# The router of a mixture of experts in five pieces, its places with five products, and a PSUM bank for each tile of an expert's output

## The chip, the cores and the metric

The kernel runs on one core of a Trainium2 chip, as one program. The metric is the device time of an execution in microseconds; lower is better. The core has TensorE for matrix products (PE in the profile), VectorE (DVE), ScalarE (ACT), GpSimd (POOL) and a queue for transfers, SyncE (SP). Each engine works through its own list of instructions; they wait for each other by semaphores. Products are written to PSUM[...] and DVE or ACT copies them out.

## The reference

The input is 8 batches of 512 tokens with 256 features. Two decoder layers follow each other, each with self-attention, attention with a context, and a feed-forward part, with a normalisation after each. The last two parts are where the change is:

```python
x = _layernorm(x + _L1_xattn_ref(x, ctx_1024, L1_xattn_Wq1, ..., L1_xattn_bo), axis=-1)
x = _layernorm(x + _L1_ffn_ref(x, L1_ffn_gamma, L1_ffn_beta, L1_ffn_router_w, L1_ffn_W1, L1_ffn_W2), axis=-1)
```

The attention with the context has 8 heads of 64 features; each token attends to the 512 tokens of its batch and 64 context tokens. The feed-forward part is a mixture of 8 experts:

```python
xn = (x - mu) * jax.lax.rsqrt(var + EPS) * gamma + beta
logits = jnp.einsum('btd,ed->bte', xn, router_w)
probs = jax.nn.softmax(logits / TEMP, axis=-1)
w, idx = jax.lax.top_k(probs, K)
wdense = jnp.sum(jax.nn.one_hot(idx, E, dtype=w.dtype) * w[..., None], axis=-2)
h = jax.nn.silu(jnp.einsum('btd,edf->betf', xn, W1))
y = jnp.einsum('betf,efd->betd', h, W2)
out = jnp.einsum('bte,betd->btd', wdense, y)
return out + res
```

With K = 2, E = 8, and 1,024 hidden features of each expert. Each token's result needs its two chosen experts only.

## The kernel before

Everything is in 32-bit floats. The core goes through the parts one after the other; in each, batches, heads and blocks of 128 tokens are the units of a software pipeline. The helper `_pipeline` (L32) runs a list of units through a list of stages with delays: in each step, one unit stands in every stage. At the end of a step it takes one function from a list of work put off (`put_off`, or `last_route` in the last part) and calls it, which puts that function's instructions at this place in the program.

**The context attention of the second layer** ("l1_context") has 8 x 4 x 4 = 128 units (batch b, pair of heads c, block of 128 tokens i). In each step TensorE makes the scores of one unit (`l1x_scores`: s_sc, L1077 and L1079), transposes the probabilities of the unit two steps earlier (`l1x_transposes`: tP2 L1092, tP L1097, each evacuated by `evac`, which takes DVE at L108 and ACT at L110 in turn), multiplies with the values of the unit six steps earlier (`l1x_values`: o_pv L1109), and does a piece of the next head pair's projections (`l1x_project`: t_qk L1034, copied by ACT into q or by DVE into k, L1039; t_v L1044), or, once per batch, the transposes of the next batch's x (`l1x_share`: xT, through tT L198). DVE takes the maxima (nm, L1081) and scales by the sums (L891, L893); ACT takes the exponentials (L1082). In this stage TensorE's instructions keep the order of the program (`tc.manual_schedule(engines={PE})`); the other engines' are ordered by the compiler's scheduler.

When the fourth head pair of a batch is done, `out_done` (L943) puts off two pieces of the output projection (`project_and_norm`: o_out L239, added to x and bias at L246, and after the second piece the normalisation `normed`, L213 to L223, whose power runs on POOL at L216), and `routed` puts off the batch's router, four pieces with an empty one ahead of each:

- `route_norm`: the experts' normalisation, into the tile `z`, which also holds the two weights of each token and its number; x doubled (L1165), and written to the array `total` in memory. The pool that holds `z` has one buffer for it.
- `route_transposes`: z is transposed (tZ, L1175) and scaled with gamma and beta on ACT (L1176) into xnT, one of the two buffers with the tag xT, which x's own transposes use too.
- `route_picks`: eight products give the logits (o_r, L1190); softmax and the two largest of eight follow on DVE with one exponential on ACT (L1198 to L1221). At L1221 the token numbers are copied into z.
- `route_places`: each chosen token's place in its expert's region is the number of tokens before it with the same choice, counted by products of the 0/1 matrix of choices `both` with a strictly triangular matrix `under` (the same block of 128 tokens) and one of ones (the blocks before): 14 products for o_rank (L1229, L1231, L1233), the last four for the new counts. Then the row numbers (irow), and eight indirect transfers, each of 128 rows, from z to the experts' input `rows_in` (L1245), issued by POOL.

Batch 6 is followed by `early_blocks`, which makes on DVE the table of which expert each of the first units has, and the load of the first unit. Batch 7 keeps its router for the next part, where `last_route` holds it, with two empty pieces after the first.

**The experts** ("l1_experts") work in 39 units, 32 pairs of 128-row tiles, in which each unit's tiles share an expert, and seven single tiles. A unit is loaded (`moe_load`: its cells of the table, xr L1368 and weights L1369 and L1370, by SP), two steps later transposed (`moe_pre`, tZ), then multiplied with the first weights (`moe_up`: s_h L1402) and the second (`moe_down`: o_y L1419). Its rows are scaled with their weights (L1439) and added to `total` by indirect transfers (L1440). The tail loads `total` (L1487), normalises it and writes it out.

PSUM in these parts: two tiles of two banks for s (s_sc, s_h), three of one bank for t (tP2, tP, tT, tZ, t_qk, t_v, and, through `u_tile`, o_out, o_r, o_rank, o_y), and one for o_pv. A tile waits until the reader of the tile that had its bank is done.

Of the kernel before, what the change touches and what calls it, by code (L numbers as in the profile page):

```python
# [11 lines left out]
F32 = mybir.dt.float32  # L12
I32 = mybir.dt.int32
AF = mybir.ActivationFunctionType
ALU = mybir.AluOpType
AX = mybir.AxisListType
PSUM = bass.MemoryType.PSUM

P = 128
S = 512  # L20
D = 256
S2 = 64
NT = S // P
# [5 lines left out]
TILES = 2  # L29
# [20 lines left out]
def decoder_kernel(ctx: ExitStack, tc: tile.TileContext, a: dict, out: bass.AP):  # L50
    nc = tc.nc
    NB = a["x"].shape[0]
    NE = a["mo_w1"].shape[0]
# [9 lines left out]
    pe, act, dve, pool, sp = nc.tensor, nc.scalar, nc.vector, nc.gpsimd, nc.sync  # L63
# [3 lines left out]
    work = ctx.enter_context(tc.tile_pool(name="work", bufs=2))  # L67
# [24 lines left out]
    def t_tile(name):  # L92
        return pp["t"].tile([P, 4, P], F32, tag="t", name=name)

    def o_tile(name):
        return pp["o"].tile([P, 512], F32, tag="o", name=name)

    def u_tile(name):

        return t_tile(name).rearrange("p i n -> p (i n)") if pp["one"] else o_tile(name)  # L100
# [89 lines left out]
    hmask, rev = small[:, 0:8], small[:, 8:16]  # L190
# [165 lines left out]
    live = {}  # L356
# [192 lines left out]
    with tc.tile_pool(name="bfly", bufs=1, side="right") as bfly, phase("l0_self") as ph, psum("a", 3, 1, 1):  # L549
# [10 lines left out]
        o = o_tile("o_wlat")  # L560
        for c in range(KC):
            for k in range(KC):
                pe.matmul(
                    o[:, c * 64 : (c + 1) * 64],
                    lhsT=wkT[:, k, c * P : (c + 1) * P],
                    rhs=wdown[:, k, :],
                    start=(k == 0),
                    stop=(k == KC - 1),
# [53 lines left out]
        o = o_tile("o_bias")  # L622
# [167 lines left out]
    with phase("l0_context_ffn") as ph:  # L790
# [10 lines left out]
        for f in range(0, 8, 2):  # L801
# [8 lines left out]
            pieces=2,  # L810
# [84 lines left out]
    put_off = []  # L895
# [103 lines left out]
    for c in range(4):  # L999
        o = u_tile("o_k2")  # L1000
        for kc in range(KC):
            pe.matmul(
                o[:, 0:NC2],
                lhsT=wk2[:, kc, c * P : (c + 1) * P],
                rhs=ctxT[:, kc, :],
                start=(kc == 0),
                stop=(kc == KC - 1),
# [124 lines left out]
    ones = keep.tile([P, P], F32, name="ones")  # L1132
    under = keep.tile([P, P], F32, name="under")
# [15 lines left out]
    def e_tile(name):  # L1149
        return work.tile([P, NT, NE], F32, tag=name, name=name, bufs=1)  # L1150

    def e_col(name):
        return work.tile([P, NT], F32, tag=name, name=name, bufs=1)

    def over_e(c):
        return c.unsqueeze(2).to_broadcast([P, NT, NE])

    def over_i(c):
        return c.unsqueeze(1).to_broadcast([P, NT, NE])
# [22 lines left out]
            )  # L1182
        live["xnT", b] = xnT

    def route_picks(b):
        xnT = live.pop(("xnT", b))
        o = u_tile("o_r")[:, 0 : NT * NE].rearrange("p (i e) -> p i e", e=NE)
        for i in range(NT):
            for c in range(KC):
                pe.matmul(  # L1190
                    o[:, i, :],
                    lhsT=xnT[:, c, i * P : (i + 1) * P],
                    rhs=rw[:, c, :],
                    start=(c == 0),
                    stop=(c == KC - 1),
                )
        pr, top, hit, rest = e_tile("pr"), e_col("top"), e_tile("hit"), e_tile("rest")
        dve.tensor_reduce(top, o, AX.X, ALU.max)  # L1198
        dve.tensor_tensor(pr, o, over_e(top), ALU.subtract)
        act.activation(pr, pr, AF.Exp, scale=1.0 / 1.5)  # L1200
        dve.tensor_reduce(top, pr, AX.X, ALU.add)
        dve.reciprocal(top, top)
        dve.tensor_tensor(pr, pr, over_e(top), ALU.mult)

        left = pr
        picks = []
        for k in range(2):
            pick = e_tile(f"pick{k}")
            dve.tensor_reduce(top, left, AX.X, ALU.max)
            dve.tensor_tensor(hit, left, over_e(top), ALU.is_equal)  # L1210
            dve.tensor_tensor(hit, hit, over_i(rev), ALU.mult)
            dve.tensor_reduce(top, hit, AX.X, ALU.max)
            dve.tensor_tensor(pick, over_i(rev), over_e(top), ALU.is_equal)
            if k == 0:
                dve.scalar_tensor_tensor(rest, pick, -2.0, pr, ALU.mult, ALU.add)
                left = rest
            picks.append(pick)
        both, z = e_tile("both"), live["z", b]
        dve.tensor_tensor(both, picks[0], picks[1], ALU.add)
        dve.tensor_tensor(z[:, :, D : D + NE], both, pr, ALU.mult)  # L1220
        dve.tensor_copy(z[:, :, D + NE], tokens_at[:, b * NT : (b + 1) * NT])  # L1221
        live["picks", b] = picks, both

    def route_places(b):

        picks, both = live.pop(("picks", b))
        o = u_tile("o_rank")
        for i in range(NT):
            pe.matmul(o[:, i * NE : (i + 1) * NE], lhsT=under, rhs=both[:, i, :], start=True, stop=(i == 0))  # L1229
            for j in range(i):  # L1230
                pe.matmul(o[:, i * NE : (i + 1) * NE], lhsT=ones, rhs=both[:, j, :], start=False, stop=(j == i - 1))  # L1231
        for i in range(NT):
            pe.matmul(o[:, NT * NE : (NT + 1) * NE], lhsT=ones, rhs=both[:, i, :], start=(i == 0), stop=(i == NT - 1))  # L1233
        rank, hit, place = e_tile("rank"), e_tile("hit"), e_col("place")
        dve.tensor_tensor(rank, o[:, 0 : NT * NE].rearrange("p (i e) -> p i e", e=NE), over_i(count), ALU.add)
        dve.tensor_tensor(rank, rank, over_i(region), ALU.add)
        dve.tensor_tensor(count, o[:, NT * NE : (NT + 1) * NE], count, ALU.add)
        z = live.pop(("z", b))
        for k in range(2):
            dve.tensor_tensor(hit, picks[k], rank, ALU.mult)  # L1240
            dve.tensor_reduce(place, hit, AX.X, ALU.add)
            row = work.tile([P, NT], I32, tag=f"irow{k}", name="irow", bufs=2)
            dve.tensor_copy(row, place)
            for i in range(NT):
                pool.indirect_dma_start(  # L1245
                    out=rows_in[:, :],
                    out_offset=bass.IndirectOffsetOnAxis(ap=row[:, i : i + 1], axis=0),
                    in_=z[:, i, :],
                    in_offset=None,
                )  # L1250
# [161 lines left out]
    def moe_down(n):  # L1412
        _, mine, size = where[n]
        h = live.pop(("h", n))
        xr, _, w2, cells = live.pop(("load", n))
        o = u_tile("o_y").rearrange("p (i n) -> p i n", i=TILES)
        for i in range(size):
            for f in range(8):
                pe.matmul(  # L1419
                    o[:, i, :],  # L1420
                    lhsT=h[:, f, i * P : (i + 1) * P],
                    rhs=w2[:, f, :],
                    start=(f == 0),
                    stop=(f == 7),
                )

        wt = ph.tile([P, TILES, NE], F32, tag="wt", name="wt", bufs=2)[:, 0:size]
        share = ph.tile([P, TILES], F32, tag="share", name="share", bufs=2)[:, 0:size]
        to = ph.tile([P, TILES], I32, tag="to", name="to", bufs=4)[:, 0:size]
        tc.keep_in_program_order(  # L1430
            dve.tensor_tensor(wt, xr[:, :, D : D + NE], mine.unsqueeze(1).to_broadcast([P, size, NE]), ALU.mult)
        )
        dve.tensor_reduce(share, wt, AX.X, ALU.add)
        tc.keep_in_program_order(dve.tensor_copy(to, xr[:, :, D + NE]))
        y = ph.tile([P, TILES, D], F32, tag="y", name="y", bufs=3)

        tc.keep_in_program_order(dve.tensor_copy(y[0:1, 0, 0:2], cells))
        for i in range(size):
            dve.tensor_scalar(y[:, i, :], o[:, i, :], share[:, i : i + 1], None, ALU.mult)  # L1439
            pool.indirect_dma_start(  # L1440
                out=total[:, :],
                out_offset=bass.IndirectOffsetOnAxis(ap=to[:, i : i + 1], axis=0),
                in_=y[:, i, :],
                in_offset=None,
                compute_op=ALU.add,
            )
# [2 lines left out]
    AHEAD = 1  # L1449

    def routed(b):
        pieces = [partial(f, b) for f in (route_norm, route_transposes, route_picks, route_places)]
        if b == NB - 1:

            last_route.extend(pieces[:1] + 2 * [nothing] + pieces[1:])
            return

        for piece in pieces:
            put_off.extend((nothing, piece))
        if b == NB - 2:  # L1460
            put_off.append(early_blocks)
            put_off.extend(partial(moe_load, n, tables_rows) for n in range(AHEAD))
# [25 lines left out]
    for b in range(NB):  # L1488
        y = ph.tile([P, NT, D], F32, tag="y_out", name="y_out", bufs=4)
# [93 lines left out]
```

## Time and profile before

| what | us |
|---|---|
| median of 3 runs (lowest, highest) | 3648.78 (3641.66, 3656.81) |
| the profiled execution: its own time | 3650.17 |
| its span in the profile | 3648.5 |
| TensorE busy | 3429.4 (94%) |
| VectorE busy | 2173.6 (60%) |
| ScalarE busy | 1437.9 (39%) |
| GpSimd busy | 1092.5 (30%) |
| mean granted TensorE clock | 0.965 |

The parts before the context attention of the second layer take some 2,250 us of the span; the context attention ends at about 3,080, the experts' products at 3,606, the rest is the tail. "Idle" of an engine is time in which its next instruction waited, put down to what came last. TensorE's products are pipelined, and the ends that the profile gives them are modelled, so the time from one start to the next says more than one record's length; each product of 32-bit floats shows as two records.

### The profile page before, as it was taken

The page shows a single profiled execution, that of the slowest core. Times are in us where ns is not written, and L with a number is a line of the kernel's source. Part 1 is how long each engine was busy: PE and PEld are TensorE (multiplying, and loading weights), DVE is VectorE, ACT ScalarE, POOL GpSimd, SP SyncE. Part 2 cuts the span into 40 slices and gives each one's busy share as a digit, 9 for nine tenths or more (in the row PEclk, how much of TensorE's full clock was granted, in tenths as well). Part 3 has the DMA queues.
Part 4 walks back from the last instruction along what each step waited for, and adds up shares of the span by engine and source line. Part 5 has one row for each costly group of instructions (what it writes and reads, how often), then busy time and mean ns, then how long its engine had stood idle before and what let it go on. Part 6 is the DMA issues. An engine that isn't in the chain of part 4 may idle for free. (4 is left out here: it accounts for less than half of the span.)

```text
span 3648.5 us, 52874 instructions
## 1 busy us (share of the span) xinstructions
PE 3429.4 (94%) x19718; PEld 2117.7 (58%) x19718; DVE 2173.6 (60%) x6158; ACT 1437.9 (39%) x2947; POOL 1092.5 (30%) x960
## 2 busy tenths in 40 slices
PE   8999999998999899999999999999999998999995
PEld 3333343345666556665666666555555555888884
DVE  5776776656666377778777885665666655200112
ACT  2444444453434254445444553433333333222222
POOL 3877777762111122222222220010101101222222
PEclk8999999998999999999999999999999999999997
DMA  4000011110000297232222330000000002766674
GB/s 132 30 24 24 24 36 33 38 60 12 4 1 1 52 270 165 36 41 36 36 36 36 41 47 4 10 13 18 20 8 21 19 13 92 230 179 190 184 229 134
DMA packets 166002, 234.97 MB, mean 64 GB/s; under 512 B 26569, under 2 KB 128649, under 8 KB 165746
## 3 DMA queue, kind: packets, MB, share of 16 engines
q1 hardware_dynamic: 139010, 175.83, 15.8%
q0 software_dynamic: 25584, 51.57, 9.4%
q8 instruction: 156, 2.56, 0.3%
q10 hardware_dynamic: 1152, 4.19, 0.3%
q14 instruction: 100, 0.82, 0.1%
HBM read 135.83 MB, written 61.11 MB: 54 GB/s over the span
## 5 line engine op out<-in xcount | busy, mean ns | idle before, releaser
L430 DVE CUSTOM_DVE_ANT_0 scored<-s_sc,decay 128x512 f32<-128x512 f32 x512 | 323.5, 687 | 221.7 <-PE s_sc L425 220.6
L861 POOL DMA_DIRECT2D qk<-turned x256 | 202.9, 1205 | 657.0 <-PE t_v L868 264.9
L483 ACT ACTIVATE pt<-s_st 128x1024 f32<-128x1024 f32 x256 | 261.1, 1023 | 262.1 <-PE s_st L479 232.9
L283 ACT ACTIVATE p<-p,nm 128x128 f32<-128x128 f32 (+3 forms) x512 | 283.1, 554 | 159.7 <-DVE nm L281 157.0
L110 ACT COPY pt<-tP 128x512 f32<-128x512 f32 (+2 forms) x416 | 205.6, 496 | 308.4 <-PE tP L939 189.4
L1082 ACT ACTIVATE p<-s_sc,nm 128x576 f32<-128x576 f32 x256 | 191.1, 747 | 342.7 <-DVE nm L1081 241.3
L893 DVE TENSOR_SCALAR p<-p,rsum 128x576 f32<-128x576 f32 (+4 forms) x768 | 295.8, 427 | 5.5
L1439 DVE TENSOR_SCALAR y<-o_y,share 128x256 f32<-128x256 f32 x71 | 31.4, 479 | 397.2 <-PE o_y L1419 397.2
L1402 PE MATMUL s_h<-xnT,we 128*128 128x256 f32 (+1 forms) x1248 | 262.1, 364 | 0.6 <-DMA we<-in_mo_w 0.6
L1081 DVE TENSOR_REDUCE nm<-s_sc 128x1 f32<-128x576 f32 x256 | 185.2, 748 | 115.4 <-PE s_sc L1079 114.0
L1419 PE MATMUL o_y<-we,h 128*128 128x256 f32 x1136 | 251.4, 379 | 0.0
L271 DVE CUSTOM_DVE_ANT_0 p<-s_sc,tabs 128x128 f32<-128x128 f32 (+3 forms) x512 | 232.6, 482 | 16.5 <-PE s_sc L907 16.5
L108 DVE COPY pt<-tP 128x512 f32<-128x512 f32 (+2 forms) x416 | 235.9, 576 | 8.0 <-PE tP L1097 3.6
L1402 PEld LDWEIGHTS s_h<-xnT,we 128*128 128x128 f32 x1248 | 218.0, 192 | 25.5 <-DMA we<-in_mo_w 1.0
L1419 PEld LDWEIGHTS o_y<-we,h 128*128 128x128 f32 x1136 | 215.3, 190 | 29.0
L1440 POOL DMA_INDIRECT total<-y,to x71 | 110.2, 1553 | 397.8 <-DVE y L1439 181.7
L907 PE MATMUL s_sc<-qk 64*128 64x128 f32 (+3 forms) x1024 | 205.8, 474 | 14.3 <-DMA qk<-turned 12.7
L939 PEld LDWEIGHTS tP<-ident,p 128*128 128x128 f32 x1280 | 136.6, 140 | 126.2 <-issue 58.4
L939 PE MATMUL tP<-ident,p 128*128 128x128 f32 x1280 | 192.5, 283 | 11.8 <-DVE pt L108 8.0
L425 PE MATMUL s_sc<-k,q 32*128 32x512 f32 x1024 | 174.5, 671 | 25.8 <-ACT pt L483 23.2
L1245 POOL DMA_INDIRECT rows_in<-z,irow x64 | 62.8, 982 | 415.4 <-DVE hit L1240 304.8
L963 PE MATMUL o_pv<-pt,vc 128*64 128x128 f32 (+1 forms) x2304 | 184.2, 293 | 0.0
(282 smaller groups left out, 6566.4 us busy)
## 6 DMA issues: line engine op xcount, KB each, us to landing
we<-in_mo_w SPq DMA_DIRECT2D x78, 1024.0 KB, 5.7
rows_in<-zero SPq DMA_DIRECT2D x64, 530.0 KB, 12.8
qk<-turned POOLq DMA_DIRECT2D x256, 128.0 KB, 4.5
coef<-in_ff_upw SPq DMA_DIRECT2D x40, 256.0 KB, 3.2
coef<-in_ff_dnw SPq DMA_DIRECT2D x40, 256.0 KB, 3.2
xr<-rows_in SPq DMA_DIRECT2D x32, 265.0 KB, 6.4
x<-in_x SPq DMA_DIRECT2D x8, 512.0 KB, 9.8
total<-x SPq DMA_DIRECT2D x8, 512.0 KB, 2.9
```

What stands on the lines that cost most here:

```text
L108: dve.tensor_copy(dst, src)
L110: act.copy(dst, src)
L271: dve.tensor_tensor_reduce(out=p[:, j, 0:n], in0=s[:, j, 0:n], in1=m, scale=1.0, scalar=-3.0e38, op0=op, op1=reduced, accum_out=mx[:, j : ...
L283: act.activation(p[:, j, 0:n], p[:, j, 0:n], AF.Exp, bias=nm[:, j : j + 1], scale=scale, accum_out=sums[:, at + j : at + j + 1],)
L430: dve.tensor_tensor_reduce(out=scored[:, h, :], in0=s[:, j, :], in1=decay[:, i, :], scale=1.0, scalar=-3.0e38, op0=ALU.mult, op1=ALU.max, ...
L483: act.activation(pt, s, AF.Exp, scale=1.0 / 16.0)
L861: pool.dma_start(out=qk[h : h + 32], in_=other[g : g + 32], accum_op=ALU.add)
L893: dve.tensor_scalar(p[:, j, 0:n], p[:, j, 0:n], rsum[:, j : j + 1], None, ALU.mult)
L907: pe.matmul(s[:, j, at : at + n], lhsT=q[h : h + 64, i * P : (i + 1) * P], rhs=k[h : h + 64, 0:n], start=True, stop=True,)
L939: pe.transpose(t[:, n, :], p[:, j, at * P : (at + 1) * P], ident)
L1402: pe.matmul(s[:, j, :], lhsT=w1[:, c, f * P : (f + 1) * P], rhs=xnT[:, c, :], start=(c == 0), stop=(c == KC - 1),)
L1419: pe.matmul(o[:, i, :], lhsT=h[:, f, i * P : (i + 1) * P], rhs=w2[:, f, :], start=(f == 0), stop=(f == 7),)
```

## The change

The router of a batch becomes five pieces: `route_odds` (logits and softmax), `route_picks` (the two largest), and the others as they were. The pieces stand otherwise: the second output projection and the router's normalisation are one function, after it an empty piece, and then one piece in each step, without empty ones between. In batch 7, too, there is a piece more. The choices have a fifth block, set to zero by POOL, so that one product with `under` covers all, and four with `ones` add the blocks before, each shifted by one block and shorter; the last eight columns get the counts of all blocks. In the experts, each of a pair's tiles has a PSUM tile of its own for o_y.

```diff
-    def route_picks(b):
+    def route_odds(b):
         xnT = live.pop(("xnT", b))
         o = u_tile("o_r")[:, 0 : NT * NE].rearrange("p (i e) -> p i e", e=NE)
...
-        pr, top, hit, rest = e_tile("pr"), e_col("top"), e_tile("hit"), e_tile("rest")
+        pr, top = e_tile("pr"), e_col("top")
         dve.tensor_reduce(top, o, AX.X, ALU.max)
...
-        both, z = e_tile("both"), live["z", b]
+        live["pr", b] = pr
+
+    def greatest(pick, left):
+
+        top, hit = e_col("top"), e_tile("hit")
+        dve.tensor_reduce(top, left, AX.X, ALU.max)
+        dve.tensor_tensor(hit, left, over_e(top), ALU.is_equal)
+        dve.tensor_tensor(hit, hit, over_i(rev), ALU.mult)
+        dve.tensor_reduce(top, hit, AX.X, ALU.max)
+        dve.tensor_tensor(pick, over_i(rev), over_e(top), ALU.is_equal)
+        return pick
+
+    def route_picks(b):
+        pr = live.pop(("pr", b))
+        rest = e_tile("rest")
+        picks = [greatest(e_tile("pick0"), pr)]
+        dve.scalar_tensor_tensor(rest, picks[0], -2.0, pr, ALU.mult, ALU.add)
+        picks.append(greatest(e_tile("pick1"), rest))
+
+        picked = work.tile([P, NT + 1, NE], F32, tag="both", name="both", bufs=1)
+        pool.memset(picked[:, NT, :], 0.0)
+        both, z = picked[:, 0:NT, :], live["z", b]
         dve.tensor_tensor(both, picks[0], picks[1], ALU.add)
         dve.tensor_tensor(z[:, :, D : D + NE], both, pr, ALU.mult)
         dve.tensor_copy(z[:, :, D + NE], tokens_at[:, b * NT : (b + 1) * NT])
-        live["picks", b] = picks, both
+        live["picks", b] = picks, picked

     def route_places(b):

-        picks, both = live.pop(("picks", b))
+        picks, picked = live.pop(("picks", b))
         o = u_tile("o_rank")
-        for i in range(NT):
-            pe.matmul(o[:, i * NE : (i + 1) * NE], lhsT=under, rhs=both[:, i, :], start=True, stop=(i == 0))
-            for j in range(i):
-                pe.matmul(o[:, i * NE : (i + 1) * NE], lhsT=ones, rhs=both[:, j, :], start=False, stop=(j == i - 1))
-        for i in range(NT):
-            pe.matmul(o[:, NT * NE : (NT + 1) * NE], lhsT=ones, rhs=both[:, i, :], start=(i == 0), stop=(i == NT - 1))
+        tiles = picked.rearrange("p i e -> p (i e)")
+
+        pe.matmul(o[:, 0 : (NT + 1) * NE], lhsT=under, rhs=tiles, start=True, stop=False)
+        for i in range(1, NT + 1):
+            n = (NT + 1 - i) * NE
+            pe.matmul(o[:, i * NE : (NT + 1) * NE], lhsT=ones, rhs=tiles[:, 0:n], start=False, stop=(i == NT))
...
-        o = u_tile("o_y").rearrange("p (i n) -> p i n", i=TILES)
-        for i in range(size):
+        os = [u_tile("o_y")[:, 0:D] for _ in range(size)]
+        for i, o in enumerate(os):
             for f in range(8):
                 pe.matmul(
-                    o[:, i, :],
+                    o,
...
         for i in range(size):
-            dve.tensor_scalar(y[:, i, :], o[:, i, :], share[:, i : i + 1], None, ALU.mult)
+            dve.tensor_scalar(y[:, i, :], os[i], share[:, i : i + 1], None, ALU.mult)
...
     def routed(b):
-        pieces = [partial(f, b) for f in (route_norm, route_transposes, route_picks, route_places)]
+        pieces = [partial(f, b) for f in (route_norm, route_transposes, route_odds, route_picks, route_places)]
         if b == NB - 1:

             last_route.extend(pieces[:1] + 2 * [nothing] + pieces[1:])
             return

-        for piece in pieces:
-            put_off.extend((nothing, piece))
+        product = put_off.pop()
+        put_off.extend([lambda: (product(), pieces[0]()), nothing] + pieces[1:])
```

## The prediction

> **What bounds the kernel now.** I read the page first, then TensorE's waits stage by stage, then the timeline around each large wait, and last the chain at the end. The page (busy time, slices, costliest groups):
>
> ```profile
> PE 3429.4 (94%) x19718; PEld 2117.7 (58%) x19718; DVE 2173.6 (60%) x6158; ACT 1437.9 (39%) x2947; POOL 1092.5 (30%) x960
> ...
> PEclk8999999998999999999999999999999999999997
> ...
> L1439 DVE TENSOR_SCALAR y<-o_y,share 128x256 f32<-128x256 f32 x71 | 31.4, 479 | 397.2 <-PE o_y L1419 397.2
> ...
> L1245 POOL DMA_INDIRECT rows_in<-z,irow x64 | 62.8, 982 | 415.4 <-DVE hit L1240 304.8
> ```
>
> TensorE is busy for 94%, so what counts is where it waits and where its clock drops. DVE's 397 us of waiting for o_y is idle time of an engine that isn't the bound: it costs nothing until the last unit. The change touches the second half only: the context stage (2250 to 3085 us in the part looked at), the experts (to 3610) and the tail (to 3648.5). TensorE's waits from 2250 to 3085:
>
> ```profile
> PE tP L1097 <- DVE k L1039: 25.4, 6, 5.6
> PE tZ L1380 <- DMA xr<-rows_in: 9.0, 1, 9.0
> PE tP L1097 <- DVE pt L108: 7.3, 6, 1.4
> PE tP L1097 <- ACT pt L110: 6.0, 6, 1.7
> ```
>
> Columns: total us, times, longest. The first falls once per batch. The timeline says why:
>
> ```profile
> 2420.96 0.96 POOL L1245 DMA_INDIRECT rows_in<-z,irow  x1 [1.82 <-DMA rows_in<-z,irow]
> 2423.53 0.17 DVE L1221 COPY z<-tokens_at 128x4 f32<-128x4 f32 x1 [5.45 <-DMA rows_in<-z,irow]
> 2423.61 0.68 DVE L1039 COPY k<-t_qk 128x512 f32<-128x512 f32 x1
> ...
> 2424.35 1.11 PE L1097 MATMUL tP<-ident,p 128*128 128x128 f32 x4 [4.16 <-DVE k L1039]
> ```
>
> So `k` isn't to blame: ahead of it on DVE stands the next batch's copy of token numbers into the one buffer of `z`, which eight row scatters, one after the other, still read. The next line shows the clock behind such a stall (stretch, five engines' busy time, granted clock):
>
> ```profile
> 2420.00:2423.50 3.50, 0.19 (x2) 0.00 (x0) 0.00 (x0) 0.00 (x0) 0.96 (x1) 1.00 0.13 44
> 2423.50:2430.30 6.80, 5.95 (x22) 4.01 (x23) 4.00 (x9) 2.04 (x5) 0.00 (x0) 0.50 0.01 2
> 2430.30:2437.00 6.70, 6.65 (x33) 3.35 (x34) 3.13 (x6) 3.38 (x8) 0.00 (x0) 1.00 0.01 1
> ```
>
> The places block is 14 products, two records each, some 111 ns apart, from 2394.76 to 2397.87:
>
> ```profile
> 2394.76 0.51 PE L1229 MATMUL o_rank<-both,under 128*128 128x8 f32 x4
> ...
> 2396.91 1.04 PE L1233 MATMUL o_rank<-both,ones 128*128 128x8 f32 x8
> ```
>
> And the end, where three scatters follow each other 4.55 us apart and the last load waits for them:
>
> ```profile
> 3601.99 0.88 DVE L1439 TENSOR_SCALAR y<-o_y,share 128x256 f32<-128x256 f32 x2 [9.53 <-PE o_y L1419]
> 3602.76 1.55 POOL L1440 DMA_INDIRECT total<-y,to  x1 [8.93 <-DVE y L1439]
> 3607.31 1.55 POOL L1440 DMA_INDIRECT total<-y,to  x1 [3.01 <-DMA total<-y,to]
> 3611.86 1.55 POOL L1440 DMA_INDIRECT total<-y,to  x1 [3.00 <-DMA total<-y,to]
> 3615.61 4.15 SPq L1487 DMA_DIRECT2D last<-total  x8
> ```
>
> [...] the half-clock stretches from 2423 to 3134 last 3.4, 6.8 or 10.2 us, 15 of them, 68 us in all. [...] the scatters here go out 2.8 to 3.4 us apart with 1.8 to 2.5 us of it waiting. [...] in the trace the pair's first scale starts only after all 16 products of o_y.
>
> **The change part by part** (profiled execution: 3650.17 us, span 3648.5).
>
> *Places.* 28 records become 10: 3.11 to about 1.1 us, −2.0 in each of eight batches. A zero fill on POOL per batch is new; nothing shows a fill that small, but POOL idles 42 us ahead of the scatters and anything up to that is hidden; its share of a wait would be under 1 us.
>
> *Order, batches 0 to 5.* Before, a batch's pieces pop at the ends of steps (1,1), (1,2), then every second step: norm (2,0), transposes (2,2), picks (3,0), places (3,2). After: second product and norm together (1,2), transposes (2,0), odds (2,1), picks (2,2), places (2,3). The scatters start three steps earlier. On the other queues, POOL's scatters pass only idle time (the next batch's bias sum still comes after them), and SP's store of 2x goes one step earlier, with nothing behind it until batch 6. Four terms:
> - The tP waits (7.3 + 6.0 = 13.3 over six batches) stand behind the transposes in (2,3): xnT can't be written before t_v has read the old xT, and the tZ banks are held meanwhile. In (2,0) a buffer is free: −13.3.
> - A new wait stands in (2,0). Its transposes need z. The two norms, now back to back on DVE with POOL's two powers between, take from the add: 0.7 + 2.0 + 0.2 + 1.3 + 1.4 + 2.0 + 0.2 + 1.2 + 1.4, about 10.5 us (rows of 2345 to 2359); the maxima and pt copies of the step queue behind z, so the bank that tZ takes comes free at about 13.2 where TensorE is ready at 10.7: +2.5 per batch, +15. Bounds 0 (maxima go first) and 5 (another scale between).
> - The next batch's copy into z also stands earlier on DVE, at the end of step (3,3), so the earlier scatters gain it little. From the scatters' row numbers to that copy I count some 19.5 us of steps; eight scatters take 22.7 to 23.9 (2400.56 to 2420.96, and 2.6 to land). DVE still waits 4.4 to 5.5. Behind it on DVE stand maxima and the pt2 copy, for which TensorE waits in (0,0): about 3.1 us (2.5 to 3.7) where it was 4.2, so −1.1, −6.6 in all.
> - Half clock. Of the 68 us, 17 in these batches follow the places blocks and about 30 the stalls. Gone or halved, half of their length returns: −11. Bounds 0 (the new wait makes as many) and −20.
>
> With places (−12), batches 0 to 5 give −12 − 13.3 + 15 − 6.6 − 11 = −28.
>
> *Batch 6.* Places −2.0 and the 6.8 us half-clock stretch at 3048, −3.4; but the tables for the early units, a long run of DVE work behind the places, now fall into (3,0) and (3,1), where maxima and copies are needed soonest: +3, from 0 if the scheduler lets those pass to 6. Net −2.4. There is no tP wait to win here.
>
> *Start of the experts.* xr went out at 3079.70, when the scatters (3054 to 3077) had landed, and TensorE waited 9.0. Three steps earlier, they land before the last o_out: −8.5. The wait's half-clock stretch, 3082.8 to 3089, is worth up to 3: −1.5.
>
> *Batch 7.* Places −2.0, half clock at 3130 −1.7. They come one unit later, and so does the first unit that needs them: the 0.38 us wait at 3159.86 stays, but six total scatters instead of three stand ahead on POOL: +1.5 (0 to 6). Net −2.2.
>
> *A bank per tile.* A pair now takes two of three banks for o_y and one for tZ. By the order each is taken again a unit later (14.35 us), and a scale takes 0.48: no wait. If that cover is gone, each pair pays up to 0.5, 16 in all. In the tail, the first scale comes after 8 products: 8 × 0.43 = 3.45 us earlier. The next two scatters follow on it, and the single's scale (3605.45) is still done before its turn at 3608.4: −3.5.
>
> Sum: −28 − 2.4 − 10 − 2.2 − 3.5 = −46. Span 3602.5, this execution 3604; the median of the runs is 1.4 below the profiled execution, so 3603.
>
> **The rivals.** *A, the stage gives back what it wins.* z comes later than I have it (5 us, +15 more) and the half clock stays (+11), table work costs 3 more: batches 0 to 5 about −2, batch 6 nothing, experts and tail −15.7; about 3631. For it: DVE is busy for 521 of the 835 us of this stage, works in order[...]. Against it: 13.3 us of waits have a plain cause that goes. *B, slower.* The scatters land later than before relative to the copy. They now run beside more of the stage's work. From 2.9 us apart to 3.9, the chain grows by 8 us, and DVE holds up TensorE by as much in each of six batches: 48 us, break-even; at 4.4 us apart +24, about 3670. For it: total's scatters take 4.55. Against: 64 of the row scatters took 2.8 to 3.4, with the same sizes and the same work around. *C, more.* No half clock is left after the places and little after the waits (another −9), and the maxima go ahead of z (−10): about 3584. That the change doesn't do what it says can be excluded for the places (the products are plainly fewer) and, by the order of instructions, for the first scale; for the copy into z it is my own reading already that little is won.
>
> **How the numbers follow.** Forecast 0.60 (own range 3590 to 3620), A 0.20, B 0.08, C 0.12. The range reaches a little past the centres of A and C: 3580 to 3636, leaving out B, some of A and of C. Half a per cent is 18 us, about what a measurement of this kernel can tell from no change: above 3630.5 is "same". Forecast, C and two fifths of A are faster: 0.80; the rest of A 0.12; B 0.08.
>
> **What would show it.** Right: o_rank about 1.1 us long; no tP wait behind tZ; TensorE's wait for xr at the first unit under 1 us; scatters of the last pair starting some 3.5 us earlier after o_y's end; a wait of 2 to 3 us in the step of the transposes; the copy into z still waiting 4 to 5.5. Wrong: scatters over 3.5 us apart, tZ or o_y waiting for a scale in the experts, half-clock stretches still summing to 60 us, or a first-unit wait for xr that stays.

## The result, and the profile after

| | before | after |
|---|---|---|
| median of the runs, us | 3652.8 (4 runs, 3641.66 to 3665.78) | 3607.06 (4 runs, 3605.43 to 3614.22) |
| ratio, 95% interval | | 0.9878 (0.9859 to 0.9897) |
| span of the profiled execution | 3648.5 | 3612.5 |

The change made the kernel 1.2% faster, 38 to 52 us by the interval. The forecast was 3603, its range 3580 to 3636, worked out from the first three runs of before (median 3648.8).

The two profiled spans differ by 36 only, and the reason isn't in the change: the first o_out of the context attention starts at 2332.5 us before and at 2345.9 after, though nothing ahead of it differs but a zero fill on POOL. Up to 2220 us the records show 129.7 us at half clock before and 160.4 after. Over all the traces below, whichever kernel, this start lies between 2332 and 2350, so below the traces are compared by landmarks: the *stage* is the time from the end of batch 0's o_out to the end of batch 7's, the *experts* go from there to the end of the last o_y, the *tail* is the rest. Within the stage each trace is taken apart into TensorE's idle time, half of the time at half clock (an estimate of what it costs: the records show a granted clock of 0.50 there, and the same scores take 1.14 us at full clock, at 2393.37 after, and 2.08 at half, at 3049.99 before), and what remains, called *work* below:

| us | stage | idle | at half clock | stage less idle, less half of half clock | experts | tail |
|---|---|---|---|---|---|---|
| before | 728.7 | 52.8 | 68.3 | 641.8 | 531.7 | 43.1 |
| after | 696.6 | 45.5 | 51.2 | 625.5 | 518.2 | 39.3 |

Between these two traces the stage gave 32.1 us (7.3 of waits, 8.5 of clock, 16.2 of work), the experts 13.5 and the tail 3.7. From the page of after (busy time, slices, groups):

```profile
PE 3410.7 (94%) x19574; PEld 2096.9 (58%) x19574; DVE 2176.7 (60%) x6158; ACT 1438.5 (40%) x2947; POOL 1095.2 (30%) x968
...
PEclk8999999997999999999999999999999999999998
...
L1446 DVE TENSOR_SCALAR y<-o_y,share 128x256 f32<-128x256 f32 x71 | 34.2, 483 | 402.5 <-PE o_y L1426 402.5
```

TensorE's waits, 2250 to 3085 us (total, times, longest):

```profile
PE tZ L1175 <- DVE pt L108: 14.6, 7, 2.3
PE t_qk L1034 <- DVE pt L108: 12.5, 4, 3.6
PE t_qk L1034 <- ACT pt L110: 9.9, 3, 5.2
PE o_pv L1109 <- DVE aT L108: 4.6, 1, 4.6
...
PE tZ L1387 <- ACT xnT L1388: 0.7, 1, 0.7
```

The clock's row hardly tells the two apart; DVE's idle time behind o_y is as long as before (402.5 us against 397.2) and costs as little. In the waits, the one for `k` and the 9.0 for xr are gone. In their place stand the predicted wait of tZ and one of t_qk. The timeline shows that the latter is the old one under a new name, the token copy behind the scatters, with the maxima and copies queued on DVE behind it:

```profile
2416.46 0.96 POOL L1252 DMA_INDIRECT rows_in<-z,irow  x1 [2.21 <-DMA rows_in<-z,irow]
...
2419.01 0.17 DVE L1228 COPY z<-tokens_at 128x4 f32<-128x4 f32 x1 [5.60 <-DMA rows_in<-z,irow]
2419.09 1.42 DVE L1081 TENSOR_REDUCE nm<-s_sc 128x1 f32<-128x576 f32 x2
...
2420.43 0.88 DVE L108 COPY pt<-tP 128x128 f32<-128x128 f32 x2
...
2420.76 3.68 PE L1034 MATMUL t_qk<-xT,q_k 128*128 128x512 f32 x4 [3.63 <-DVE pt L108]
```

That t_qk takes 3.68 us, where it takes 1.98 at full clock; it runs at the half clock that follows the wait (granted clock 0.50 from 2420.8 to 2424.2). The places, with their 40, 32, 24, 16 and 8 columns, and the end:

```profile
2392.26 0.31 PE L1237 MATMUL o_rank<-both,under 128*128 128x40 f32 x2
2392.41 1.04 PE L1240 MATMUL o_rank<-both,ones 128*128 128x32 f32 x8
2393.37 1.14 PE L1077 MATMUL s_sc<-k,q 64*128 64x512 f32 x4
```

```profile
3567.09 1.54 POOL L1447 DMA_INDIRECT total<-y,to  x1 [5.49 <-DVE y L1446]
...
3571.52 1.54 POOL L1447 DMA_INDIRECT total<-y,to  x1 [2.90 <-DMA total<-y,to]
...
3576.07 1.54 POOL L1447 DMA_INDIRECT total<-y,to  x1 [3.00 <-DMA total<-y,to]
3579.87 3.92 SPq L1494 DMA_DIRECT2D last<-total  x8
```

The first of the last three scatters goes out 5.7 us before the last o_y record (3572.8), where it was 2.3 us before it (3602.76 and 3605.03).

### The profile page after: what moved, and what is told of

It is laid out like the page before. It is cut to its first block, busy times and chain, and to the rows that moved or that the text cites. A ratio compares the mean times of both kernels' runs of the same rounds, so it can differ in the third digit from the quotient of the medians.

```text
span 3612.5 us, 52624 instructions
## 1 busy us (share of the span) xinstructions
PE 3410.7 (94%) x19574; PEld 2096.9 (58%) x19574; DVE 2176.7 (60%) x6158; ACT 1438.5 (40%) x2947; POOL 1095.2 (30%) x968
## 5 line engine op out<-in xcount | busy, mean ns | idle before, releaser
L1446 DVE TENSOR_SCALAR y<-o_y,share 128x256 f32<-128x256 f32 x71 | 34.2, 483 | 402.5 <-PE o_y L1426 402.5
L891 DVE RECIPROCAL rsum<-sums 128x2 f32<-128x2 f32 x384 | 62.9, 164 | 159.6 <-ACT p L283 93.6
```

## The experiments

The theory: places, order and banks each give what the prediction's terms say, independently, and the copy of the token numbers is what still holds the stage up. The runs are called e1 to e11; the rivals are stated with each. The runs of the kernel before beside these had medians of 3651.4 to 3653.2 us; each ratio is against those, with its 95% interval.

**The five products alone (*e1*)** (before with these and their zero block):

```diff
-        both, z = e_tile("both"), live["z", b]
+        picked = work.tile([P, NT + 1, NE], F32, tag="both", name="both", bufs=1)
+        pool.memset(picked[:, NT, :], 0.0)
+        both, z = picked[:, 0:NT, :], live["z", b]
...
-        for i in range(NT):
-            pe.matmul(o[:, i * NE : (i + 1) * NE], lhsT=under, rhs=both[:, i, :], start=True, stop=(i == 0))
...
+        pe.matmul(o[:, 0 : (NT + 1) * NE], lhsT=under, rhs=tiles, start=True, stop=False)
```

> The kernel before with only the five products for the places (and their zero block); order and o_y as before. If the half-clock stretches at 2508.9, 2618.1, 2730.7, 2843.4, 3048.2 and 3130.1 of the kernel before came from the blocks of 28 small records, as the prediction had it: 2.0 us x 8 = 16 less for the records, and up to 13.6 less for these stretches (27.2 us at half speed), so 22 to 30 us less than before, and no half-clock stretch beginning at an o_rank block. The rival: those stretches come whatever is in the block, and only the 16 us go. The wait behind the token copy (25.4 us in six batches) and the 9.0 us for xr stay under both.

Measured: 3640.82, ratio 0.9959 (0.9941 to 0.9977), 8 to 22 us less, where I had expected 22 to 30. The work left in the stage is 625.7 us, 16.0 less than before, so the records gave what they should. No half-clock stretch begins at one of the eight o_rank blocks. Yet the half clock of the stage fell only to 54.6 us: the stretches behind k became longer (6.8 us each at 2537, 2647, 2753, 2862 and 2968). And the experts took 537.9 us, 6.2 more than before, with a second wait for xr (13.2 us in the two, against 9.0 and 0.38) and one of 3.2 for weights. The total favours the rival's 16, the absence of stretches at the blocks the theory; e10 below settles it.

**The order alone (*e2*)** (the changed kernel with fourteen products and one o_y tile per pair):

```diff
-        pe.matmul(o[:, 0 : (NT + 1) * NE], lhsT=under, rhs=tiles, start=True, stop=False)
...
+        for i in range(NT):
+            pe.matmul(o[:, i * NE : (i + 1) * NE], lhsT=under, rhs=both[:, i, :], start=True, stop=(i == 0))
...
-        os = [u_tile("o_y")[:, 0:D] for _ in range(size)]
+        o = u_tile("o_y").rearrange("p (i n) -> p i n", i=TILES)
```

> The changed kernel with the fourteen products and one o_y tile per pair again, so that only the order of the router's pieces is new. By the prediction's terms: 13.3 us of tP waits and some 8 us of small waits go, 12.5 us for z and some 22 us behind the token copy stand in place of the latter's 25.4, and 9.0 us for xr go; 15 to 20 us less than before, and half-clock stretches of about 27 us behind the o_rank blocks still there. The rival, that the order is what pays and the places only ride on it: 30 us less or more. The other, that order is a wash: within 5 us of before outside the 9 us of xr.

Measured: 3628.83, ratio 0.9923 (0.9901 to 0.9945), 20 to 36 us less: more than expected, near the rival. The waits are those of the changed kernel (14.7 for tZ), with 38.1 us of idle time in the stage, six of the eight blocks of fourteen have half clock behind them, and the experts take 519.7. Idle time in the stage fell by 14.7 us where the expectation's terms come to some 12, and the experts gave 12.0 where it had the 9.0 of xr alone: half clock there fell from 13.7 to 3.4 us with that wait. (The small waits for the odd copy, 11.1 us in the stage before, fell to about half; the prediction hadn't counted them, this expectation had.)

**The banks alone (*e3*):**

```diff
-        o = u_tile("o_y").rearrange("p (i n) -> p i n", i=TILES)
-        for i in range(size):
+        os = [u_tile("o_y")[:, 0:D] for _ in range(size)]
+        for i, o in enumerate(os):
```

> The kernel before with a PSUM tile for each of a pair's tiles, and nothing else. The prediction: the first of the last three scatters to total goes out 3.45 us earlier and nothing else moves, so 3.5 us less than before. The rival, that three banks are too few when a pair takes two: waits of tZ or o_y for a scale in the experts, up to 0.5 us in each of 32 pairs, 12 us more than before on balance. A third: the last load waits for something else and nothing is won.

Measured: 3650.47, ratio 0.9992 (0.998 to 1.0003). The interval doesn't tell 3 us from none, but the landmarks do: the tail is 39.4 us here and 39.3 in the changed kernel, 43.0 to 43.1 in the four traces with one tile per pair (before, e1, e2, e4). No wait of tZ or o_y for a scale shows in the experts (530.1 us against 531.7). The prediction holds, the rival doesn't. This trace is also a second one of the stage of before, whose code is the same: 720.8 us, with 51.2 at half clock where the other had 68.3. So a difference of 8 us between two single stages is no finding, and the 8.5 us of clock between the first two traces aren't one either.

The three parts add up: 0.0041 + 0.0077 + 0.0008 = 0.0126, where the change gave 0.0122, with some 0.002 of uncertainty in each of the larger ones.

**The copy of the token numbers kept in its place (*e4*)**, in the kernel before, which is no part of the change:

```diff
-        dve.tensor_copy(z[:, :, D + NE], tokens_at[:, b * NT : (b + 1) * NT])
+        tc.keep_in_program_order(dve.tensor_copy(z[:, :, D + NE], tokens_at[:, b * NT : (b + 1) * NT]))
```

> The kernel before, with one edit that is no part of the change: the copy of the token numbers into z keeps its place in the program, behind the product of choices and weights, so that DVE doesn't come to it while the previous batch's scatters still read z. If this copy is what holds TensorE up and what the half clock follows: the 25.4 us behind k go, and of the half-clock stretches behind it (6.8, 3.4, 3.4, 6.8, 6.8: 27.2 us) up to 13.6 us of lost time; 30 to 39 us less than before. The rival, that the 5 us of DVE's wait only stand where DVE or POOL would be late anyway: under 12 us less, and another wait of 2 us or more in each batch's last step or the next one's first.

Measured: 3617.51, ratio 0.9897 (0.9873 to 0.992), 29 to 46 us less, as expected: one line is worth about as much as the whole change. Its waits, 2350 to 3070 us:

```profile
PE tZ L1380 <- DMA xr<-rows_in: 8.9, 1, 8.9
PE tP L1097 <- DVE pt L108: 7.3, 6, 1.4
PE tP L1097 <- ACT pt L110: 6.0, 6, 1.7
PE t_qk L1034 <- ACT pt L110: 4.5, 8, 0.9
```

The k wait is gone and none took its place; idle time fell by 25.4 us, from 52.8 to 27.4, and half clock from 68.3 to 34.1.

**The same in the changed kernel (*e5*):**

> The changed kernel with the same one edit: the copy of the token numbers keeps its place. In the changed kernel 22.4 us of TensorE's waits stand behind this copy in six batches and 4.6 in the last, with 30.6 us of half clock at them (15 lost). If the copy is their cause, up to 42 us less than the changed kernel, at least the 27 us of waits: 3565 to 3580. The rival, that the scatters' place in the order is what counts and the changed order left little behind the copy: under 10 us less.

Measured: 3566.82, ratio 0.9772 (0.9749 to 0.9796). That is 40 us under the changed kernel, within the 3565 to 3580 expected, and less than either edit gives alone. The stage takes 652.8 us with 20.0 of idle time and 10.2 at half clock. TensorE's waits, 2250 to 3160 us:

```profile
PE tZ L1175 <- DVE pt L108: 14.6, 7, 2.3
PE tZ L1387 <- DMA xr<-rows_in: 3.2, 2, 3.0
PE t_v L1044 <- ACT pt L110: 2.6, 5, 0.6
```

**The transposes two steps later (*e6*)** (in the changed kernel):

```diff
-        put_off.extend([lambda: (product(), pieces[0]()), nothing] + pieces[1:])
+        put_off.extend([lambda: (product(), pieces[0]()), nothing, nothing, nothing] + pieces[1:])
```

> The changed kernel with two more empty pieces ahead of the transposes, so that they stand in step (2,2) as before, odds in (2,3), picks in (3,0), places in (3,1). If the tP waits came from the transposes in (2,2) ahead of t_v in (2,3), they come back (some 13 us in six batches, with the small ones up to 20), and the wait of tZ for z (14.6 us in seven) goes; the scatters still land before the last o_out, so the wait for xr stays away. Within 8 us of the changed kernel either way. The rival, that five pieces in a row suffice wherever they stand: no tP waits, and 12 us or more less than the changed kernel.

Measured: 3667.95, ratio 1.0033 (1.0018 to 1.0048): 61 us more than the changed kernel, where I had expected 8 at most. The waits moved as expected, and three more came:

```profile
PE o_pv L1109 <- DVE aT L108: 20.0, 5, 5.4
PE s_sc L1077 <- ACT p L1082: 12.0, 7, 1.8
PE tP L1097 <- DVE pt L108: 8.7, 8, 1.4
PE t_qk L1034 <- DVE pt L108: 7.3, 2, 4.2
PE o_r L1190 <- ACT xnT L1176: 6.9, 12, 0.9
PE tP L1097 <- ACT pt L110: 6.7, 7, 1.7
```

(2350 to 3110 us.) But idle time rose only from 45.5 to 63.7 us. The half clock rose from 51.2 to 126.3: 37.6 us of the stage's 61.4.

**The same with the copy kept in place (*e11*)**, to see whether the copy was what made it slow:

> The kernel with the transposes two steps later, now with the copy kept in place. With the copy as the scheduler placed it, that was 61 us slower than the changed kernel, where I had expected 8 at most. If the copy was the cause (DVE waited 44.6 us for scatters), this is within 12 us of the changed kernel with the copy kept. If small waits and their half clock are (s_sc 12.7, tP 13.3 and o_r 6.9 us of waits, and stretches of 6.8 us behind them), most of the 61 stays: 30 us more or above.

Measured: 3627.94, ratio 0.9934 (0.9917 to 0.9951), 59 us more than the changed kernel with the copy kept. So it isn't the copy. The stage is 704.8 us against 652.8: idle 37.0 against 20.0, half clock 61.4 against 10.2 (25.6 us lost), and 9.4 us of remaining work that I can't place. The order in the timeline tells where the short waits come together:

```profile
2379.85 0.66 PE L1097 MATMUL tP<-ident,p 128*128 128x128 f32 x4 [1.44 <-DVE pt L108]
2381.18 0.66 PE L1097 MATMUL tP<-ident,p 128*128 128x128 f32 x4 [0.68 <-ACT pt L110]
2381.77 1.67 PE L1109 MATMUL o_pv<-pt,vc 128*64 128x512 f32 x4
2383.37 3.07 PE L1044 MATMUL t_v<-v_k,xT 128*128 128x128 f32 x16
...
2386.48 1.45 ACT L1176 ACTIVATE xnT<-tZ,gb 128x512 f32<-128x512 f32 x2 [5.35 <-PE t_v L1044]
...
2387.31 0.39 PE L1190 MATMUL o_r<-rw,xnT 128*128 128x8 f32 x2 [0.87 <-ACT xnT L1176]
2387.98 2.30 PE L1190 MATMUL o_r<-rw,xnT 128*128 128x8 f32 x14 [0.28 <-ACT xnT L1176]
...
2390.21 2.09 PE L1077 MATMUL s_sc<-k,q 64*128 64x512 f32 x4
```

xnT waits for t_v, as the prediction had it for the old order, but now o_r stands right behind t_v and waits for xnT too; the scores that follow take 2.09 us where they take 1.14 at full clock. In the changed kernel xnT has a free buffer, and none of this is there: ScalarE doesn't wait ahead of any of its 16 records, and o_r never waits for it. How the half clock divides between the waits and the eight-column products of o_r isn't shown: the 3.4 us ahead of its start at 2388.9 hold 1.15 us of waits and 1.36 of these products.

**The order once more, with the copy kept (*e8*)** (the kernel before with five products, a bank per tile and the kept copy: all but the order):

> The kernel before with the five products, a bank per tile and the copy kept in place: all of the change but the order of the pieces. By adding up: the five products and the banks give some 18 us, the copy some 36, so 50 us or more less than before, about 3598, less what the two count twice in half clock. Against the changed kernel with the copy kept, it shows what the order is worth by itself once no copy waits: the 9 us for xr, 13 of tP and 7 of small waits against 14.6 of tZ, so 14 to 20 us more than that kernel. The rival: the order's gain was only that the scatters ended sooner before the copy, and then the two are within 9 us (xr).

Measured: 3596.64, ratio 0.9838 (0.9811 to 0.9864), as added up. Against the changed kernel with the copy kept (0.9772) the order is worth 24 us, give or take some 13: more than the 9 of xr, so it isn't only the scatters' earlier end, and no clear miss of the 14 to 20 expected. The stage is 669.2 against 652.8 (7.9 of idle time, 5.1 lost to half clock, 3.4 of the rest), the experts 530.8 against 520.3.

**The fourteen products, with the copy kept (*e10*)** and all else as changed:

> The changed kernel with the copy kept in place and the fourteen products back: against the changed kernel with the copy kept, it measures what the fourteen cost where nearly no other half clock is left. The records: 2.0 us in each of eight batches, 16 us. If a block of 28 records with eight columns each brings the half clock by itself, a stretch of 3.4 or 6.8 us follows in most batches (27 to 40 us of them, 14 to 20 lost), and this kernel is 30 to 36 us slower than the one with the copy kept and the five products. The rival, that the stretches need a wait nearby: 16 us slower.

Measured: 3585.83, ratio 0.9838 (0.9819 to 0.9858), 24 us more than with five, give or take some 11, so the total alone doesn't decide between the two expectations. The stage does: 25.3 us more in seven batches, 11.7 of work and 27.3 more at half clock (13.7 lost), with idle time the same (19.9 and 20.0). The eighth block's gain, in the experts, goes: with five products a wait of 3.0 us for xr stands there. This is the block itself, without a wait in it or in the 1.8 us before it, and what follows (stretch, five engines' busy time, granted clock):

```profile
2481.90:2485.10 3.20, 3.20 (x32) 3.18 (x30) 0.00 (x0) 0.58 (x1) 0.00 (x0) 1.00 0.00 0
2485.80:2489.20 3.40, 3.40 (x17) 2.44 (x15) 2.71 (x8) 1.73 (x6) 1.04 (x1) 0.50 0.11 40
2489.20:2492.60 3.40, 3.40 (x12) 1.19 (x10) 1.27 (x3) 1.13 (x3) 1.44 (x2) 1.00 0.11 40
```

And the same place in the changed kernel with the copy kept, its five products first:

```profile
2475.90:2477.10 1.20, 1.20 (x14) 1.18 (x14) 0.02 (x1) 0.59 (x1) 0.00 (x0) 1.00 0.00 0
2477.10:2484.00 6.90, 6.90 (x38) 3.63 (x39) 4.84 (x16) 2.86 (x7) 2.17 (x3) 1.00 0.11 39
```

Over all traces, a half-clock stretch begins between the start and 5 us after the end of 28 of the 40 blocks of fourteen (before, e2, e3, e4, e10) and of none of the 64 of five (after and the other seven). In four of the 28 (batch 7's in before, e2, e4 and e10) TensorE doesn't wait in the block or in the 7 us ahead of it. The rival is out.

Why not in all 40? In each trace every half-clock stretch begins on one grid of 3.413 us, to within 3 ns (34 stretches in the trace of before and 34 in that of after, these to within 1 ns), and all but the last, in the tail, last whole steps of it. The blocks of fourteen can be sorted by how much of each falls into one step of this grid. With 2.3 us or more (21 blocks) a stretch at half clock follows every time, with 1.92 or less (nine) never, between them seven times in ten. In the trace of before these shares are 2.06, 2.21, 2.31, 2.39, 2.46 and 2.96 us in the six blocks that have half clock behind them, and 1.66 and 1.72 in the two that don't. The blocks of five, with none in 64, are at most 1.28 us long. That is a count over these traces; what in a block sets the clock they don't show. If a block of 3.19 us may start anywhere on the grid, it puts more than 2.1 us (the middle between 1.92 and 2.3) into one step in some 70% of cases (an estimate from these lengths): 28 of 40. By this estimate it is largely chance which batches are hit, and so is much of the difference in half clock between two traces of the same code (68.3 us before, 51.2 in e3).

**The router's normalisation on ScalarE (*e9*)**, with the copy kept:

```diff
-        normed(z[:, :, 0:D], xs[b])
+        normed(z[:, :, 0:D], xs[b], on_act=True)
```

> The changed kernel with the copy kept in place, and the router's normalisation into z done by ScalarE (four activations with scale and bias, after one small product on VectorE) in place of four operations on VectorE. If tZ's wait (14.6 us in seven batches) comes from the maxima and the copy of pt2 standing behind z on VectorE, which itself waits 0.9 us for POOL's power, it falls from 2.3 to under 1 us a batch: 9 to 14 us less than the changed kernel with the copy kept. The rival, that z itself is late whoever writes it: tZ waits as before, for z or for ScalarE, and the exponentials behind z on ScalarE cost as much again.

Measured: 3578.59, ratio 0.9797 (0.978 to 0.9814): 9 us more than with z on VectorE, by intervals that overlap; the stage takes 655.0 us, as before the edit (652.8). The wait of tZ went to 0.3 us in all, and one of t_qk for a copy of pt on VectorE came, 16.0 us in seven. So both expectations failed: the wait moved, and as a whole it neither shrank nor stayed with z. On VectorE the small product that ScalarE's form needs (L218) waits 0.9 us for POOL's power, as z did, and the maxima behind it begin 9.5 us after o_out's end where they began 10.9 us after it (means of seven batches). So writing z seems a small part of that time; the statistics of the two normalisations and two powers remain. Why t_qk meets the wait here and tZ there I haven't settled.

**Batch 7's odds and picks in one piece (*e7*)**, with the copy kept:

```diff
-            last_route.extend(pieces[:1] + 2 * [nothing] + pieces[1:])
+            last_route.extend(pieces[:1] + 2 * [nothing] + [pieces[1], lambda: (pieces[2](), pieces[3]()), pieces[4]])
```

> The changed kernel with the copy kept in place, and batch 7's odds and picks in one piece, so that its places stand one unit of the experts earlier, as in the kernel before. If the 2.66 us wait for xr in the seventh unit came from that one unit, it falls to under 0.5 us and this is 2 us less than the changed kernel with the copy kept alone; no other wait changes. The rival, that the wait is made by the total scatters ahead of the row scatters on POOL: it stays above 1.5 us.

Measured: 3563.89, ratio 0.9762 (0.9738 to 0.9786), not to be told from the 3566.82 without it. The wait for xr is 3.6 us, so it isn't the number of pieces. The first unit that needs these rows moves with the places. The row scatters stand between those to total on POOL in both (from 3056.73 to 3079.67 here); that they are what makes xr late is argued from this order, not shown by a run.

## Why the prediction was right

The time (3607.06 against 3603) and the sign were right. The terms came to −46; by landmarks it is −49.3 against the trace of before and −39.8 if the stage and the experts of before are taken from the trace of the banks (e3), whose stage is the same code and whose experts waited no more. That the sum fits so well is in part luck: two terms were wrong by some 6 us each, the small waits and batch 6, and they cancel. Term by term:

- *Places*: right. The block is 1.18 us where it was 3.19, −2.0 each. That a record of up to 40 columns takes no longer than one of eight was my estimate; in the trace of after the ten records of a block start 102 ns apart, where the 28 of before start 109 apart (means of a block without a wait in it).
- *tP waits*: right, and shown: they go with the old order (after, e2, e5) and come back with the transposes in (2,2) (e6, e11), in the same two places of a batch (1.44 + 0.68 us in the one shown).
- *The wait for z*: right in place and size, 1.7 to 2.3 us against 2.5, in the seventh batch too, where I hadn't put it. That VectorE's queue makes it and not z itself agrees with the run with z on ScalarE: TensorE waits about as long (16.0 us in seven batches against 14.6), for a copy that stands in that queue.
- *The copy into z*: the mechanism right, DVE's waits 4.85 to 6.75 us against 4.4 to 5.5 (before, they were 3.9 to 6.9). TensorE waited 21.7 us in six batches, −3.7 where I had −6.6; in batches 2 and 3 it was 5.2 and 4.0, over my bound of 3.7.
- *Half clock*: −8.5 us in the stage against −14.4 for batches 0 to 6, and nothing against the trace of the banks, so its size isn't shown by these traces. That the blocks of fourteen bring it was right; with the copy kept they cost 13.7 us in seven batches (e10). Of the 13 stretches left in the stage six (20.5 us) begin within 2 us of the end of a wait of tZ and the other seven behind the copy: half clock came behind six of the new wait's seven, too, which the term had only as its bound. The "68 us in all" of the prediction is wrong: the 15 stretches it lists add up to 81.6, and 68 leaves out the last two. The term was worked out from those in batches 0 to 5, so it doesn't move.
- *Small waits*: not counted, worth some 6 us.
- *Batch 6*: wrong. From its own o_out to batch 7's it takes 74.6 us where it took 70.5: +4.1 against −2.4. The failed step is "Net −2.4", which looked at the tables and not at the copy: batch 7's copy waits for batch 6's scatters as any other. Before, it did so at 3079.81, while TensorE waited for xr anyway. Three steps earlier it stands ahead of aT, and TensorE waits. With the copy kept (e5) the same stretch takes 68.7 us:

```profile
3040.26 0.41 SPq L1375 DMA_DIRECT2D xr<-rows_in  x1
...
3040.36 0.17 DVE L1228 COPY z<-tokens_at 128x4 f32<-128x4 f32 x1 [5.50 <-DMA rows_in<-z,irow]
...
3040.44 0.69 DVE L108 COPY aT<-o_pv 128x512 f32<-128x512 f32 x1
...
3041.18 5.75 PE L1109 MATMUL o_pv<-pt,vc 128*64 128x512 f32 x16 [4.59 <-DVE aT L108]
```

- *Experts and batch 7*: −13.5 against −12.2. The 9.0 us are gone (xr goes out at 3040, the products need it at 3054.9); the seventh unit waits 2.66 us, where I had 0.38 + 1.5.
- *Tail*: −3.7 against −3.5; shown alone by the banks.

Of the rivals, A had z later and the half clock staying: z came as forecast, and 51.2 us of half clock did stay in the stage. B needed scatters 3.9 us apart; in the stage they took 2.7 to 4.0, 3.0 on average. Single ones over 3.5 were to be a sign of being wrong, but before the change they took 2.7 to 4.5 and the same 3.0 on average; the prediction's 2.8 to 3.4 left out the longer ones (the waiting in them reached 3.58 us, where it had 2.5). C had the half clock gone after the places, which it is, and the waits' with it, which it isn't.

## What to carry to other kernels

Here the compiler's scheduler put an instruction that needs nothing computed before it, a copy of constants, ahead of its turn. Its destination was still being read, so it blocked all of DVE's queue behind it (for 5.60 us at 2419.01 after), and the profile put the wait down to whatever stood next (here k, pt or aT). Follow such a wait one instruction further back on the engine: one line that kept the copy in place was worth as much as the whole change, and on top of it as much again.

When pieces are moved, look at each batch's end too: a wait that cost nothing because a longer one covered it (DVE's 4.46 us at 3079.81 before, under the 9.0 for xr) costs when that one goes (4.59 us of TensorE's at 3041.18 after).

## What the hardware showed

In all 13 traces here the half-clock stretches begin in steps of 3.413 us (34 of them before, 34 after). A block of 28 records with eight columns each is followed by 3.4 to 6.8 us of half clock in 28 of 40 cases, though in most of them TensorE doesn't wait in it at all; that holds for each of the 21 cases in which 2.3 us or more of the block fall into one step of the grid. Ten records with 8 to 40 columns never are (0 of 64).

Short waits came with a loss beyond their length: with the transposes later and the copy kept, 16.9 us more of idle time, mostly in waits of 0.3 to 1.8 us, came with 25.6 us lost to half clock (an estimate, half of the 51.2 more at half clock; e11 against e5, and some of that goes with the products of o_r). A sum of waits alone would have missed most of a loss of 60 us.
